# Second-layer routing tables built from one token tile at a time, with four buffers and later matmuls

## The chip, the cores and the metric

The kernel runs on one core of a Trainium2 chip. The metric is the device time of one launch in microseconds (us). The kernel before takes 1202.62 us (median of three runs, 1202.22 to 1203.43).

## The reference

Two transformer layers work on 4 x 512 tokens of width 256, all in float32. Each layer adds an attention part and a mixture-of-experts part, both computed from the same normalised input. The change is in the mixture of experts of the second layer: 7 experts, the best 3 of them for each token.

```python
def _L1_ffn_ref(x, W1, Wg, W2, Ws1, Wsg, Ws2, gate_w, gate_b, biases):
    output = _expert_ffn(x, Ws1, Wsg, Ws2)
    gate_probas = jax.nn.softmax(x @ gate_w + gate_b, axis=-1)
    _, topk_idxs = jax.lax.top_k(gate_probas + biases, TOP_K)
    topk_probas = jnp.take_along_axis(gate_probas, topk_idxs, axis=-1)
    topk_probas = topk_probas / jnp.sum(topk_probas, axis=-1, keepdims=True)
    for e in range(NUM_ROUTED):
        w_e = jnp.sum(topk_probas * (topk_idxs == e), axis=-1)
        output = output + _expert_ffn(x, W1[e], Wg[e], W2[e]) * w_e[..., None]
    return output
...
xn = _layernorm(x, axis=-1)
x = x + _L0_attn_ref(xn, ...) + _L0_ffn_ref(xn, ...)
xn = _layernorm(x, axis=-1)
x = x + _L1_attn_ref(xn, ...) + _L1_ffn_ref(xn, ...)
```

## The kernel before

**Experts by slots.** The 2048 tokens are 16 tiles (NT) of 128. Each token goes to 3 experts (K1), and the rows that go to one expert are packed into slots of 128 rows; there are 54 slots (NS1). Two tables are needed for that: for every slot and lane the number of the token that sits there (from it idx1, the row to gather, and to1, the row to add to) and the share with which its result counts (part1). `route1` (L1460) makes them.

**How the tables are made.** For every pair of a token and one of its three choices, the lane and the slot are known. VectorE compares the lane with 0 to 127 (row, L1538) and the slot with 0 to 53 (the left half of col, L1546). GpSimd multiplies col by the share (right half, L1552) and then by the token's number (left half, L1555). TensorE multiplies row by col and adds all 48 products of 128 x 108 up in one bank, ix (L1529); a product is issued as two matmuls. The kernel before does two token tiles at a time: 8 rounds of 6 products, in two buffers each of row and col; the products of a round are issued one round after its comparisons. At the end VectorE turns ix into the tables (L1561 to L1564).

**The order around it.** The order of the instructions on TensorE, VectorE and ScalarE is written out by hand. From the first attention unit on, the main loop goes over 32 units (4 batches x 8 units), in each over 4 tiles of 128 queries, and for each tile over two half-steps. A half-step issues the two score matmuls of a unit that comes two units later (`score_max`, L940, into the only tile pa), the two score matmuls of this unit (`score`, L979), the row maximum on VectorE (`take_max`, L958), whatever `after` (L832) held back for VectorE, and the exponentials on ScalarE (L994). The first half-step of a tile also issues the products with the values of the tile before (`values`, L1002). I call it an A-half, and the other one a B-half. Then come fillers: pieces of other work, each a generator that yields an estimate of its time.

- While the tables aren't ready, `piece` gives one filler a half-step, and the list todo (with `route1` in it) is advanced by `within`, up to a `yield None`.
- Afterwards `pieces_for` gives fillers by a credit of 0.87 in an A-half and 1.5 in a B-half.
- `slots1` (L1219) is the filler for the experts. For slot s: `tokens(s)` puts a ScalarE copy of the transposed rows, xT (L145), and starts a transposition for slot s+2 on SP's queue and a gather for slot s+4 on GpSimd's queue (L1230); two gate halves (`half`, L1258) in the one bank "g"; their products with the activation on VectorE (L1174, L1175), held back by `after` until the next half-step; two transpositions (`turn_back`, L1240); two down products (`down`, L1271), a ScalarE copy y with the share (L1281), and a GpSimd scatter that adds y to rows in DRAM (L1283). The first gate half of the next slot waits for the step that `behind` (L811) gives: the next A-half.
- `project_out` (L1154) is the attention's output projection, four tiles of two products each (L1138), added by VectorE one half-step later (L1142).
- Fillers other than the gate halves share two banks ("f"); `takes` (L815) hands them out.

**The end.** When the last slot is done, `sums1` (L1338) reads the summed expert rows back (L1350 on GpSimd's queue, which waits for the last scatter), adds them (L1359), and `leaves` (L1146) stores a finished batch (L1151, on SP's queue, which is in order). On the same queue `context` sends the sums of a unit's exponentials away (L1020, L1024) and `quotients` their reciprocals (L1033, L1035) and reads them back spread out (L1039). `closing` (L1044) multiplies with them (L1095 on GpSimd) and makes the last projections (L1106 to L1126).

**Weights.** When `route1` has ended, `expert_weights` loads the last experts' 2304 KB on GpSimd's queue (L762), into the room that the tables were worked out in.

Of the kernel before, what the change touches and what calls it, by code (L numbers as in the profile page):

```python
# [11 lines left out]
F32 = mybir.dt.float32  # L12
# [9 lines left out]
P = 128  # L22
# [9 lines left out]
NT = B * NQ  # L32
# [8 lines left out]
E1, F1, K1 = 7, 256, 3  # L41
W1E = HC * 2 * F1 + HC * H
NS1 = (NT * P * K1 + E1 * (P - 1)) // P
# [5 lines left out]
def two_layer_kernel(  # L49
# [123 lines left out]
    def numbers(pool, n: int):  # L173

        lane = counting(pool, P, 1, 0, "lane")
        slot = counting(pool, n, 1, 0, "slot")
        tok = counting(pool, NT, P, 1, "tok")
        full = counting(pool, NT, P, 0, "full")
        return lane, slot, tok, full, tok[:, 0:1]

    def triangle(pool):

        ones = pool.tile([P, P], F32, tag="ones", name="ones")
        nc.gpsimd.memset(ones, 1.0)
        before = pool.tile([P, P], F32, tag="before", name="before")
        nc.gpsimd.affine_select(
            out=before,
            in_=ones,
            compare_op=ALU.is_gt,
            fill=0.0,  # L190
            base=0,
            pattern=[[1, P]],
            channel_multiplier=-1,
        )
        return ones, before
# [124 lines left out]
    def softmax(lg, n: int, pool, name: str, nq: int = NQ):  # L320

        mx = pool.tile([P, nq], F32, tag="mx", name=f"mx{name}")
        nc.vector.reduce_max(out=mx, in_=lg, axis=AX.X)
        d = pool.tile([P, nq, n], F32, tag="sd", name=f"sd{name}")
        nc.vector.tensor_tensor(d, lg, mx.unsqueeze(2).to_broadcast([P, nq, n]), ALU.subtract)
        nc.scalar.activation(d, d, AF.Exp)
        sm = pool.tile([P, nq], F32, tag="sm", name=f"sm{name}")
        nc.vector.reduce_sum(out=sm, in_=d, axis=AX.X)
        nc.vector.reciprocal(sm, sm)
        return d, sm.unsqueeze(2).to_broadcast([P, nq, n])  # L330
# [12 lines left out]
    with tc.tile_pool(name="w0", bufs=1, side="right") as w0:  # L343
# [37 lines left out]
        with tc.tile_pool(name="rt", bufs=1) as rt, tc.tile_pool(name="a0", bufs=2) as a0, tc.tile_pool(  # L381
            name="a0p", bufs=2, space=PSUM
# [229 lines left out]
            for i in range(NT + 2):  # L612
                b, t = divmod(i, NQ)
# [40 lines left out]
        for i in range(2):  # L654
            k = hp.tile([P, 2, 2, S], F32, tag=f"k{i}", name=f"k1_{i}")
# [22 lines left out]
        with tc.tile_pool(name="m0", bufs=3) as m0, tc.tile_pool(  # L678
            name="m0p", bufs=2, space=PSUM, reuse_waits="tile"
# [113 lines left out]
    with tc.tile_pool(  # L793
        name="a1", bufs=2, side="right", reuse_waits="tile"
    ) as a1, tc.tile_pool(
        name="a1p", bufs=1, space=PSUM, reuse_waits="tile"
    ) as a1p:
        def filler(shape, name: str):

            return a1p.tile(shape, F32, tag="f", name=name, bufs=2)  # L800
# [659 lines left out]
        def route1():  # L1460


            kept = Room(ew, LATE * W1E, E1 * W1E, hp)
            lane, slot, tok, full, own = numbers(kept, NS1)
            toks = kept.tile([P, NT, K1], F32, tag="toks", name="toks1")

            nc.gpsimd.tensor_scalar(
                toks, tok.unsqueeze(2).to_broadcast([P, NT, K1]), 1.0, None, ALU.add
            )
            place1 = kept.tile([P, NT, K1], I32, tag="place1", name="place1")  # L1470
            share1 = kept.tile([P, NT, K1], F32, tag="share1", name="share1")
            spare_row = kept.tile([P, 1], F32, tag="spare", name="spare_row")
            nc.gpsimd.tensor_scalar(spare_row, own, float(NT * P + 1), None, ALU.add)
            for i in range(2):
                kept.tile([P, NT, K1], F32, tag=f"pf{i}", name=f"pf{i}")
            rt = Room(ew, kept.at, E1 * W1E, hp)
            ones, before = triangle(rt)
            yield 0.1
            lb = rt.tile([P, NT, E1], F32, tag="lb", name="lb1")
            nc.vector.tensor_tensor(  # L1480
                lb, va1[:, :, KV1:VG], gb1s.unsqueeze(1).to_broadcast([P, NT, E1]), ALU.add
            )
            e, rs = softmax(lb, E1, rt, "1", NT)
            yield 1.6
            pr = rt.tile([P, NT, E1], F32, tag="pr", name="pr1")
            nc.vector.tensor_tensor(pr, e, rs, ALU.mult)
            pads = 8 - K1
            bp = rt.tile([P, NT, E1 + pads], F32, tag="bp", name="bp1")
            nc.gpsimd.memset(bp[:, :, E1 : E1 + pads], PAD1)
            nc.vector.tensor_tensor(  # L1490
                bp[:, :, 0:E1], pr, eb1s.unsqueeze(1).to_broadcast([P, NT, E1]), ALU.add
            )
            yield 0.6
            mask = yield from top_of(rt, bp, E1, pads, K1, PAD1, PAD1, 4)
            flat = mask.rearrange("p t e -> p (t e)")
            yield 0.3
            pc = filler([P, 2, NT * E1], "cnt1")
            nc.tensor.matmul(pc[:, 0, :], ones, flat, start=True, stop=True)
            nc.tensor.matmul(pc[:, 1, :], before, flat, start=True, stop=True)
            yield None  # L1500
            cnt = rt.tile([P, 2, NT * E1], F32, tag="cnt", name="cnt1s")
            nc.vector.tensor_copy(cnt, pc)
            yield 0.4
            for i, tag in enumerate(("rest", "bp")):
                rt.held["sel", i] = rt.held[tag, 0]
            part = yield from spots(
                rt, kept, E1, K1, W1E, mask, pr, cnt, own, full, place1, share1, off1
            )
            yield 0.9
            while not free:  # L1510
                yield None


            rt = Room(ew, kept.at, E1 * W1E, hp)
            ix = gate_bank([P, 2 * NS1], "ix1")
            n, last = 2 * K1, NT // 2 - 1
            which, rows, toks, parts = (
                x.rearrange("p t k -> p (t k)") for x in (*part, toks, share1)
            )

            def spread(x, t: int, m: int):
                return x[:, ts(t, n)].unsqueeze(2).to_broadcast([P, n, m])

            held = []
            for t in range(last + 2):
                if held:
                    row, col = held.pop()
                    for k in range(n):
                        nc.tensor.matmul(  # L1529
                            ix,  # L1530
                            row[:, k, :],
                            col[:, k, :],
                            start=t == 1 and k == 0,
                            stop=t == last + 1 and k == n - 1,
                        )
                if t <= last:
                    row = rt.tile([P, n, P], F32, tag="row", name=f"row1_{t}", bufs=2)
                    nc.vector.tensor_tensor(  # L1538
                        row,
                        lane.unsqueeze(1).to_broadcast([P, n, P]),  # L1540
                        spread(rows, t, P),
                        ALU.is_equal,
                    )
                    col = rt.tile([P, n, 2 * NS1], F32, tag="col", name=f"col1_{t}", bufs=2)
                    lanes = col[:, :, 0:NS1]
                    nc.vector.tensor_tensor(  # L1546
                        lanes,
                        slot.unsqueeze(1).to_broadcast([P, n, NS1]),
                        spread(which, t, NS1),
                        ALU.is_equal,  # L1550
                    )
                    nc.gpsimd.tensor_tensor(  # L1552
                        col[:, :, NS1:], lanes, spread(parts, t, NS1), ALU.mult
                    )
                    nc.gpsimd.tensor_tensor(lanes, lanes, spread(toks, t, NS1), ALU.mult)  # L1555
                    held.append((row, col))
                    yield 1.1
                    yield None
            number = ix[:, 0:NS1]
            none = rt.tile([P, NS1], F32, tag="none", name="none")  # L1560
            nc.vector.tensor_scalar(none, number, 0.0, spare_row, ALU.is_equal, ALU.mult)  # L1561
            nc.vector.scalar_tensor_tensor(to1, number, -1.0, none, ALU.add, ALU.add)
            nc.vector.tensor_scalar(idx1, number, -1.0, 0.0, ALU.add, ALU.max)
            nc.vector.tensor_copy(part1, ix[:, NS1:])  # L1564
            yield 0.8
# [17 lines left out]
        with tc.manual_schedule(engines={ENG.PE, ENG.DVE, ENG.Activation}):  # L1583
# [57 lines left out]
            for g in range(AHEAD):  # L1641
                b, u = units[g]
                for t in range(NQ):
                    out, pa = banks(b, u, t)
                    for s in range(4):
# [4 lines left out]
                            start=True,  # L1650
                            stop=True,
# [91 lines left out]
            held = {}  # L1743
# [3 lines left out]
            todo, last, urgent = [], [], []  # L1747
# [56 lines left out]
            for g, (b, u) in enumerate(units):  # L1804
# [17 lines left out]
                for t in range(NQ):  # L1822
                    exs = {}
                    if nxt:
                        for first, second in ((0, 2), (2, 0)):
# [18 lines left out]
                            if b == 0:  # L1844
                                chore((last,))
                                n = joined
# [4 lines left out]
                    else:  # L1851
                        chore()
                        out, _ = banks(b, u, t)
                        for s in range(4):
# [4 lines left out]
                                start=True,  # L1859
                                stop=True,  # L1860
# [111 lines left out]
```

## Time and profile before

| what | value |
|---|---|
| median of three runs | 1202.62 us |
| the profiled execution | 1206.58 us |
| its span in the profile | 1204.6 us |
| TensorE matmuls busy | 1118.2 us (93%) |
| VectorE busy | 659.7 us (55%) |
| ScalarE busy | 530.1 us (44%) |
| GpSimd busy | 379.7 us (32%) |
| L1538, 8 times, 594.7 to 620.4 us | 0.948 us each |
| L1546, 8 times | 0.490 us each |
| L1552 and L1555, 8 times each | 0.731 and 0.733 us each |
| L1529, 96 matmuls, 599.4 to 624.8 us | 0.275 us each |
| first and last gate half L1258 | 638.5 and 1149.3 us |

In lines of a timeline the columns are the start and the length in us, the engine (PE is TensorE, PEld its weight loads, DVE VectorE, ACT ScalarE, POOL GpSimd, SPq the instructions that issue DMAs on SP's queue), the line, the operation, what it writes and reads, how many were merged, and in brackets how long the engine was idle just before and what ended that. In a list of waits it is the engine and line that waited, what it waited for, the total in us, how often, and the longest single wait. In a line of a windows view it is the stretch, its length, the busy time of PE, PEld, DVE, ACT and POOL with the number of instructions, then the granted TensorE clock, the busy share of the DMA engines and GB/s.

### The profile page before, as it was taken

What the parts mean: (1) busy time and instruction counts of PE and PEld (TensorE: products, weight loads), DVE (VectorE), ACT (ScalarE), POOL (GpSimd) and SP (SyncE); (2) the same over time, 40 slices, a digit from 0 to 9 for tenths busy, and PEclk for the clock granted to TensorE, in tenths of its full rate; (3) what the DMA queues carried; (4) which work ended last, traced back from release to release, by engine and by line L of the source; (5) the groups of instructions that cost most, each with busy time, mean ns of one, the idle gap of its engine ahead of it and who ended that gap; (6) DMA issues with size and microseconds to landing.
All of it is one profiled execution on the core that took longest, in us unless ns stands there. A gap on an engine that the chain in (4) does not pass through costs nothing.

```text
span 1204.6 us, 17284 instructions
## 1 busy us (share of the span) xinstructions
PE 1118.2 (93%) x5608; PEld 518.4 (43%) x5608; DVE 659.7 (55%) x1329; ACT 530.1 (44%) x1088; POOL 379.7 (32%) x403
## 2 busy tenths in 40 slices
PE   6889989999999988898899999999999999999996
PEld 4456656777765533332243233333233333333333
DVE  3387434444444488757665445555555555555544
ACT  3421233333411103444335545666556566556662
POOL 4400254434334657200042232323133232333140
PEclk9898999999999989899999999999999999999999
DMA  9400268878821322420013332333232323223242
GB/s 355 184 1 1 57 171 187 185 167 178 165 72 57 115 69 85 136 49 9 10 53 100 48 61 44 56 54 57 37 61 52 56 47 60 53 41 53 35 100 64
DMA packets 129863, 101.83 MB, mean 85 GB/s; under 512 B 92048, under 2 KB 117424, under 8 KB 129136
## 3 DMA queue, kind: packets, MB, share of 16 engines
q1 hardware_dynamic: 109296, 58.62, 20.3%
q0 software_dynamic: 19488, 41.70, 15.5%
q8 instruction: 47, 0.77, 0.3%
q10 hardware_dynamic: 992, 0.41, 0.1%
q14 instruction: 40, 0.33, 0.1%
HBM read 51.42 MB, written 26.20 MB: 64 GB/s over the span
## 4 chain that ended last, share of the span: by engine, by line
PE 73%; DVE 15%; DMA 5%; issue 3%; POOL 2%; ACT 1%; SPq 0%; POOLq 0%; ACTq 0%; DVEq 0%
PE pa L940 19%; DVE mx L958 9%; PE po L1002 8%; PE pg L711 7%; PE pg L1258 7%; PE py L735 5%; PE ps L1380 4%; PE py L1271 3%; PE pb L979 2%; PE po L598 2%; PE sc L565 2%; DMA xh<-xg 2%; PE pys L1394 1%; PE pa L727 1%; PE ph L1188 1%
## 5 line engine op out<-in xcount | busy, mean ns | idle before, releaser
L958 DVE TENSOR_REDUCE mx<-pa 128x2 f32<-128x1024 f32 x247 | 302.5, 1225 | 295.8 <-PE pb L979 270.1
L994 ACT ACTIVATE ex<-pb 128x512 f32<-128x512 f32 x496 | 269.6, 595 | 284.9 <-PE pb L979 275.4
L940 PE MATMUL pa<-k,q 32*128 32x512 f32 x960 | 272.1, 643 | 25.7 <-DVE mx L958 20.7
L979 PE MATMUL pb<-q,k 32*128 32x512 f32 x960 | 273.1, 643 | 0.0
L940 PEld LDWEIGHTS pa<-k,q 32*128 32x128 f32 x960 | 72.2, 184 | 162.9 <-DVE mx L958 108.0
L1283 POOL DMA_INDIRECT sum_rows<-y,place x54 | 85.1, 1575 | 166.9 <-ACT y L1281 152.1
L1002 PE MATMUL po<-ex,v 128*32 128x512 f32 x1024 | 137.3, 608 | 0.0
L685 POOL DMA_INDIRECT xg<-xn_rows,idx x79 | 74.9, 948 | 154.1 <-DMA xh<-xg 70.2
L1258 PE MATMUL pg<-ew,xT 128*128 x216 | 116.3, 620 | 3.6 <-ACT xT L145 1.6
L1230 POOL DMA_INDIRECT xg<-xn_rows,idx x54 | 53.9, 998 | 185.9 <-DMA xh<-xg 158.8
L711 PE MATMUL pg<-we,xT 128*128 x316 | 106.9, 460 | 4.3 <-ACT xT L145 4.3
L145 ACT COPY xT<-xh 128x512 uint16<-128x512 uint16 x133 | 89.1, 670 | 15.9 <-DMA xh<-xg 11.2
L735 PE MATMUL py<-we,aT 88*128 x316 | 81.3, 380 | 0.0
L1410 POOL DMA_INDIRECT yk<-y_rows,place x64 | 61.9, 968 | 49.6 <-DVE x L1440 33.5
L979 PEld LDWEIGHTS pb<-q,k 32*128 32x128 f32 x960 | 73.3, 184 | 0.2 <-ACT ex L994 0.2
L722 DVE TENSOR_TENSOR a<-sg,pg 128x176 f32<-128x176 f32 x79 | 26.6, 337 | 83.3 <-ACT sg L720 73.3
L711 PEld LDWEIGHTS pg<-we,xT 128*128 128x128 f32 x316 | 59.4, 190 | 26.9 <-ACT xT L145 5.8
L720 ACT ACTIVATE sg<-pg 128x176 f32<-128x176 f32 x79 | 25.1, 317 | 100.9 <-PE pg L711 83.5
L1271 PE MATMUL py<-ew,aT 128*128 x216 | 65.5, 412 | 0.0
L1002 PEld LDWEIGHTS po<-ex,v 128*32 128x32 f32 x1024 | 20.2, 108 | 98.2 <-issue 96.3
L1271 PEld LDWEIGHTS py<-ew,aT 128*128 128x128 f32 x216 | 35.5, 189 | 57.7 <-issue 30.9
L735 PEld LDWEIGHTS py<-we,aT 88*128 88x128 f32 x316 | 53.7, 190 | 4.6 <-issue 0.2
(262 smaller groups left out, 1380.0 us busy)
## 6 DMA issues: line engine op xcount, KB each, us to landing
y_rows<-y SPq DMA_DIRECT2D x79, 128.0 KB
we<-in_dram SPq DMA_DIRECT2D x4, 2432.0 KB
ew<-in_dram SPq DMA_DIRECT2D x5, 768.0 KB
ew<-in_dram POOLq DMA_DIRECT2D x1, 2304.0 KB
xg<-xn_rows,idx POOLq DMA_INDIRECT x133
xh<-xg SPq DMA_TRANSPOSE x133
x<-in_dram SPq DMA_DIRECT2D x4, 512.0 KB
xn_rows<-xs POOLq DMA_DIRECT2D x16, 128.0 KB
```

Of the source, the lines that this page charges most:

```text
L145: nc.scalar.copy(xT.rearrange("p c t -> p (c t)").bitcast(U16).rearrange("p (c t a) -> p c t a", c=HC, a=2), xh.rearrange("p a c t -> p c ...
L685: nc.gpsimd.indirect_dma_start(out=xg, out_offset=None, in_=xn_rows[:, :], in_offset=bass.IndirectOffsetOnAxis(ap=idx[:, s : s + 1], axis=0),)
L711: nc.tensor.matmul(pg, xT[s][:, c, :], we[:, ds(regs[s] + c * 2 * F0, 2 * F0)], start=c == 0, stop=c == HC - 1,)
L735: nc.tensor.matmul(py, actT[s][0:F0H, j, :], we[0:F0H, ds(regs[s] + HC * 2 * F0 + j * H, H)], start=j == 0, stop=j == 1,)
L940: nc.tensor.matmul(pas[i], q[at : at + ST, u, ts(t, P)], k[at : at + ST, 0, u % 2, :], start=True, stop=True, tile_position=(at, 0),)
L958: nc.vector.reduce_max(out=m[:, s0 : s0 + 2, t], in_=pa, axis=AX.X)
L979: nc.tensor.matmul(pb, k[at : at + ST, 1, u % 2, ts(kc, P)], q[at : at + ST, u, :], start=True, stop=True, tile_position=(at, 0),)
L994: nc.scalar.activation(ex, pb, AF.Exp, scale=1.0 / math.sqrt(D1))
L1002: nc.tensor.matmul(po[ts(s, ST), :], v[:, kc, half * 4 + s, :], exs[s], start=kc == 0, stop=kc == NQ - 1, tile_position=(0, s * ST),)
L1258: nc.tensor.matmul(pg, xT[s][:, c, :], ew[:, ds(regs[s] + c * 2 * F1, 2 * F1)], start=c == 0, stop=c == HC - 1,)
L1271: nc.tensor.matmul(py, x[:, f, :], ew[:, ds(regs[s] + HC * 2 * F1 + f * H, H)], start=f == 0, stop=f == HC - 1,)
L1283: nc.gpsimd.indirect_dma_start(out=sum_rows[:, :], out_offset=bass.IndirectOffsetOnAxis(ap=to1[:, s : s + 1], axis=0), in_=y, in_offset=No ...
```

## The change

The loop goes over 16 single token tiles in place of 8 pairs, with 3 products each. Row and col have four buffers each. The products of tile t are issued in the round of tile t+3, in front of that tile's comparisons, and only every second round ends a half-step (`yield 1.1` and `yield None`). So a half-step issues the products of two tiles and the comparisons of two others. The loop has 19 rounds in place of 9.

```diff
-            n, last = 2 * K1, NT // 2 - 1
+            n, last = K1, NT - 1
...
             held = []
-            for t in range(last + 2):
-                if held:
-                    row, col = held.pop()
+            for t in range(last + 4):
+                if t > 2:
+                    row, col = held.pop(0)
                     for k in range(n):
                         nc.tensor.matmul(
                             ix,
                             row[:, k, :],
                             col[:, k, :],
-                            start=t == 1 and k == 0,
-                            stop=t == last + 1 and k == n - 1,
+                            start=t == 3 and k == 0,
+                            stop=t == last + 3 and k == n - 1,
                         )
                 if t <= last:
-                    row = rt.tile([P, n, P], F32, tag="row", name=f"row1_{t}", bufs=2)
+                    row = rt.tile([P, n, P], F32, tag="row", name=f"row1_{t}", bufs=4)
...
-                    col = rt.tile([P, n, 2 * NS1], F32, tag="col", name=f"col1_{t}", bufs=2)
+                    col = rt.tile([P, n, 2 * NS1], F32, tag="col", name=f"col1_{t}", bufs=4)
...
                     held.append((row, col))
-                    yield 1.1
+                    if t % 2:
+                        yield 1.1
+                if t % 2:
                     yield None
```

## The prediction

> **What bounds the kernel now.** Sums are made on the profiled execution: span 1204.6 us inside 1206.58 us; the runs' median is 1202.62, and the change in microseconds is carried over to it.
>
> The page's chain of the work that ended last comes first: TensorE, with its score line L940, leads it, and DVE is second by the maximum L958, which must leave the one PSUM tile that the next L940 writes.
>
> ```profile
> PE 73%; DVE 15%; DMA 5%; issue 3%; POOL 2%; ACT 1%; SPq 0%; POOLq 0%; ACTq 0%; DVEq 0%
> ```
>
> So I cut the trace into half-steps, from one L940 pair to the next. An A-half also holds the value products L1002, a B-half doesn't; the fillers come on top. Without fillers a half-step never falls under 2.46 us (594.86 to 597.32): L940, then L958, then L940 again. With them TensorE's work decides. The second view is the timeline where the table is built, L1529:
>
> ```profile
> 604.19 0.70 PE L940 MATMUL pa<-k,q 32*128 32x512 f32 x2
> 606.32 1.59 PE L1529 MATMUL ix<-ew 128*128 128x108 f32 x12
> 607.84 0.70 PE L940 MATMUL pa<-k,q 32*128 32x512 f32 x2
> 609.60 1.59 PE L1529 MATMUL ix<-ew 128*128 128x108 f32 x12 [0.62 <-POOL ew L1555]
> 611.12 0.70 PE L940 MATMUL pa<-k,q 32*128 32x512 f32 x2
> ```
>
> The A-half (604.19 to 607.84) is full. The B-half (to 611.12, 3.28 us) waits 0.62 us for GpSimd's L1555. The list of TensorE's waits between 594 and 640 us gives the whole prize:
>
> ```profile
> PE ix L1529 <- POOL ew L1555: 2.5, 4, 0.6
> ```
>
> The 11.0 us that the line's own view shows there are mostly weight loads waiting beside other matmuls.
>
> Third, two misfits in the expert part, when a filler comes a half-step too close to what it needs:
>
> ```profile
> 689.08 0.70 PE L940 MATMUL pa<-k,q 32*128 32x512 f32 x2
> 691.84 0.42 DVE L1175 SCALAR_TENSOR_TENSOR act<-ths,pg 128x256 f32<-128x256 f32 x1
> 692.40 1.10 PE L1258 MATMUL pg<-ew,xT 128*128 x2 [0.46 <-DVE act L1175]
> ...
> 700.53 0.67 ACT L145 COPY xT<-xh 128x512 uint16<-128x512 uint16 x1
> 701.26 1.13 PE L1258 MATMUL pg<-ew,xT 128*128 x2 [0.71 <-ACT xT L145]
> ```
>
> Misfit one: a slot's first gate half stands in the A-half right after the B-half with the previous slot's second; the bank is free only after L958, L1174 and L1175. That A-half takes 4.35 us (689.08 to 693.43; again 4.36 from 707.33), and 3.56 with the same matmuls and an earlier second half (836.96 to 840.52): 0.79 us. Misfit two: L145 is issued in the same B-half as the gate half that reads it. It takes 3.98 us (698.34 to 702.32; again from 902.34) against 2.99 (1083.38 to 1086.37): 0.99 us.
>
> Last, the end:
>
> ```profile
> 1169.83 0.42 SPq L1151 DMA_DIRECT2D out_dram<-x  x1
> 1170.35 0.57 SPq L1020 DMA_DIRECT2D sums<-o  x1
> 1176.34 0.35 DVE L1033 RECIPROCAL sums<-sums 128x32 f32<-128x32 f32 x1 [5.44 <-DMA sums<-o]
> 1182.76 2.33 POOL L1095 TENSOR_TENSOR cr<-cr,den 128x1024 f32<-128x1024 f32 x1 [4.96 <-DMA den<-quot]
> 1185.15 1.34 PE L1106 MATMUL last<-wo1s,cr 128*128 128x256 f32 x4 [2.87 <-POOL cr L1095]
> ```
>
> ```profile
> 1187.00:1189.00 2.00, 2.00 (x9) 0.52 (x8) 0.59 (x2) 0.00 (x0) 0.00 (x0) 0.50 0.00 0
> ```
>
> The store L1151 holds SP's queue until the expert sums are added; L1020 behind it feeds L1033, the quotients, L1095 and L1106. TensorE stands 2.87 us, and the granted clock falls to 0.50 (the last line is of the windows view; the clock is the third number from its end).
>
> **The change, part by part.** The order of instructions of both kernels shows the same 96 table matmuls, spread over nine half-steps (3, seven times 6, 3) in place of eight of 6; every filler after that comes one half-step later; A and B change places for most experts.
>
> *Wait for L1555.* Each half-step now multiplies a token tile that was compared two half-steps before and one that was the first of the last: ready about 1.4 us early. With all four B-halves at 2.66 (3.28 less 0.62): -2.5. The four buffers bring no new wait: the second comparison starts about 3.05 us into an A-half (L958 begins at 1.2 and takes 1.1 from start to start, the first pair 0.7), the product that frees its buffer ends near 2.9.
>
> *Twice as many instructions.* DVE's 768 elements take 0.948 us and 324 take 0.49, so about 0.15 is fixed; from start to start a half-step's four take 1.42 in place of 1.32. With L958 that is 2.6, under the pair's mean of 3.15. GpSimd's 0.73 for 324 elements halves nearly, since its 1024 take 2.33. But GpSimd now multiplies while DVE compares the next tile, which it didn't before. One row shows what that can do: L1086 takes 1.85 us beside L1095, 0.29 otherwise. Bounds: nothing, or two GpSimd multiplications of 0.37 in DVE's way in each half-step, 0.24 to 0.4 per pair beyond the slack, 1.7 in all. I take +0.5, nearer the lower end, since DVE has some 0.5 us to spare per half-step. [...]
>
> *Half-steps' shapes.* Fillers are the same, so only those under 2.46 differ. Pricing each half-step by the trace's shortest of the same contents, the first group of three saves 0.75, the 188 from 624.98 to 1157.65 differ by +0.1, and the last down product L1271 (1.05) falls behind them: +0.4.
>
> *Start of the experts.* The tables are done about 0.5 us earlier, so the first L145 ends near 637.9 in place of 638.46: it waits for its transposition, which shares the DMA engines with the 2304 KB of weights. TensorE gets to the first gate half at 636.7 and waits 1.2 (before: 0.3). +0.95, between 0 and 1.2.
>
> *Misfits.* I list for every slot in which half-step its copy, gate halves and products stand. Before, misfit one comes twice (beside the very first pair of slots, equal in both) and misfit two twice, and these are the slots where the trace has the waits. After: six times (slots 26, 28, 30, 32, 34, 52) and four times (31, 33, 35, 37). Four more at 0.79 and two more at 0.99: +3.2 and +2.0. A third is new: in two places both first output projections (L1138) stand in one B-half and take both filler banks, so the third must wait in the next A-half for L958 and the addition L1142: 1.2 + 1.1 + 0.4 + 0.1 = 2.8 against 2.1. No row shows it: 0 to 0.75 each. The same bank rule costs L1258 in full, so I take 0.7: +1.4.
>
> So far: -2.5 + 0.5 + 0.4 + 0.95 + 3.2 + 2.0 + 1.4 = +5.95.
>
> *The end.* From the start H of the last regular A-half (before 1157.65): the last slot's scatter moves from H+0.5 to H+4.0, since its product now stands behind the A-half's 2.1 us. Its loads and the first eight additions follow 11.6 us later as before, H+15.6. The eight sums and copies now stand before the store on SP and land by H+14.3, so L1033 runs at H+15.7 (before H+18.7). But the quotient is now behind the 512 KB store: traffic after that store lasted 4 us, so H+20.3; the reading back takes up to 4.5 as before, and L1095 2.4: L1106 may go at H+26.4 to 27.3. TensorE is there at H+25.7 (before 24.6). It waits 0.7 to 1.6 in place of 2.87: -1.7. The clock rows 1185 to 1191 (0.74, 0.50, 0.91) cost 0.52 + 1.0 + 0.18 = 1.7; by the stretched matmuls 1.55. A wait of 1.32 us at 597.32 left the clock at 1.00, so the dip goes: -1.55, or nothing. [...]
>
> Sum: +5.95 - 1.7 - 1.55 = +2.7, and 1202.62 + 2.7 = 1205.3 us.
>
> **Rivals.** (1) Faster: the misfits in the expert part cost nothing in the new order, as DVE and ACT run ahead of TensorE there. Without the 6.6 us of misfits 1198.7; it decides once these cost under about 1.5 us. For: the wait on L1555 goes, and the stall at the end. Against: the order shows the same neighbours that cost 0.79 and 0.99 in all four cases of before. (2) No change: the third misfit and the wait at the experts' start don't show: 1205.3 - 1.4 - 0.95 = 1203.0. For: no row shows either. [...] (4) The table wait stays: +2.5, 1207.8; the order speaks against it.
>
> **How the numbers follow.** Forecast 0.46; (1) 0.11; (2) 0.22; (3) 0.14; (4) 0.07. 0.2% is 2.4 us, about what runs between 1202.22 and 1203.43 can tell from no change; the limit is 1205.0, so my forecast lies just beyond it. I give a third of its chance, with (2), to no change: faster 0.11, same 0.37, slower 0.52. The range reaches down by the costs that no row shows (1.4 and 0.95) and the end's remaining wait (1.1), and up to rival 3: 1201.9 to 1209.2.
>
> **What would show it.** [...] L1258 waiting for L1175 in six A-halves and for L145 in four B-halves between 900 and 1150; L1138 waiting for L1142 twice. L1020 ahead of L1151; L1106 waiting under 1.6 us, the clock at 1.00 after it. I am wrong if the misfits are absent while their order stands, or if the end's gain outgrows them.

## The result and the profile after

| | before | after |
|---|---|---|
| median of 22 runs each | 1202.07 us (1197.73 to 1206.06) | 1206.06 us (1201.86 to 1208.05) |
| ratio after to before | | 1.003, 95% interval 1.0021 to 1.0039 |
| profiled execution, its span | 1206.58, 1204.6 us | 1206.52, 1204.7 us |

The change costs 4.0 us by the medians. The two profiled executions are level only by chance: they differ by 3.48 us before the change begins (the first half-step to start after the first comparison has begun starts at 594.86 before, at 591.38 after). The page's chain of the work that ended last reaches back only to 1159.08 us in the changed kernel, about 4% of the span, and can't be set beside the one of before. So I count from that half-step on, in half-steps from one first L940 pair to the next. The boundaries are read from the timelines: 12 half-steps of table building, 6 with the gate halves of the first two slots, 180 to the last score pair L940, and the rest.

| stretch | before | after | difference | the prediction's terms |
|---|---|---|---|---|
| first comparisons, 12 half-steps | 38.83 | 35.40 | -3.43 | -2.5 + 0.5 - 0.75 = -2.75 |
| the next 6, start of the experts | 18.27 | 22.17 | +3.90 | +0.95 |
| the next 180, the misfits and L1271 | 507.76 | 514.85 | +7.09 | 3.2 + 2.0 + 1.4 + 0.1 + 1.05 = +7.75 |
| from there to the end of the span | 44.88 | 40.90 | -3.98 | -1.7 - 1.55 = -3.25 |
| sum | 609.74 | 613.32 | +3.58 | +2.7 |

First the tables, in TensorE's timeline of the changed kernel (start, duration, engine and line, what it writes and reads, then any wait in brackets):

```profile
601.75 1.59 PE L1529 MATMUL ix<-ew 128*128 128x108 f32 x12
603.27 0.70 PE L940 MATMUL pa<-k,q 32*128 32x512 f32 x2
...
604.34 1.59 PE L1529 MATMUL ix<-ew 128*128 128x108 f32 x12
605.86 0.70 PE L940 MATMUL pa<-k,q 32*128 32x512 f32 x2
...
607.92 1.59 PE L1529 MATMUL ix<-ew 128*128 128x108 f32 x12
609.44 0.70 PE L940 MATMUL pa<-k,q 32*128 32x512 f32 x2
```

No bracket is left: the 0.62 us for L1555 is gone. From 603.27 to 605.86 a B-half takes 2.59 us where it took 3.28, and the A-half to 609.44 takes 3.58.

Then TensorE's list of waits from 560 us on (what waited, for whom, sum in us, times, the longest):

```profile
PE pg L1258 <- ACT xT L145: 6.4, 6, 2.3
PE pg L1258 <- ACT y L1281: 2.8, 5, 0.6
...
PE po L1138 <- DVE x L1142: 1.3, 2, 0.6
...
PE pg L1258 <- DVE act L1175: 0.5, 1, 0.5
```

These are the misfits: 5 + 1 of the first kind, four of the six waits for L145 of the second, two of the third. One of each kind in the timeline:

```profile
904.73 0.42 DVE L1175 SCALAR_TENSOR_TENSOR act<-ths,pg 128x256 f32<-128x256 f32 x1
904.78 0.47 ACT L1281 ACTIVATE y<-py,share 128x256 f32<-128x256 f32 x1 [0.50 <-PE py L1271]
...
905.30 1.10 PE L1258 MATMUL pg<-ew,xT 128*128 x2 [0.56 <-ACT y L1281]
```

```profile
892.98 0.74 DVE L1142 TENSOR_TENSOR x<-x,po 128x256 f32<-128x256 f32 x2
...
893.44 1.13 PE L1138 MATMUL po<-wo1s,cr 128*128 128x256 f32 x4 [0.65 <-DVE x L1142]
...
948.39 1.13 PE L1258 MATMUL pg<-ew,xT 128*128 x2 [0.71 <-ACT xT L145]
```

The bracket at 905.30 names L1281, but L1281 reads the filler bank, not the gate bank. L1175, which frees the gate bank, ends at 905.15, and L1258 starts 0.15 us later, as it does where L1175 is named (939.54, L1175 ended 939.40). The half-steps around these waits last 4.36, 3.84 and 3.97 us.

The other two of the six waits for L145 stand at the start of the experts:

```profile
635.77 3.14 PE L1258 MATMUL pg<-ew,xT 128*128 x4 [2.27 <-ACT xT L145]
...
642.74 1.13 PE L1258 MATMUL pg<-ew,xT 128*128 x2 [1.28 <-ACT xT L145]
```

The windows view of the same place (stretch, its length, busy time of PE, PEld, DVE, ACT and POOL, then the granted clock, the DMA share and GB/s):

```profile
636.00:637.00 1.00, 1.00 (x3) 0.26 (x3) 0.00 (x0) 0.70 (x2) 0.67 (x1) 0.73 0.16 23
637.00:638.00 1.00, 1.00 (x3) 0.33 (x1) 0.00 (x0) 0.00 (x0) 0.61 (x1) 0.50 0.62 120
638.00:639.00 1.00, 1.00 (x6) 0.17 (x5) 0.00 (x0) 0.06 (x1) 0.88 (x2) 0.50 0.62 143
639.00:640.00 1.00, 1.00 (x8) 0.35 (x8) 0.00 (x0) 0.33 (x1) 0.08 (x1) 0.57 0.49 141
```

TensorE waits 2.27 us, and 0.7 us after the wait's end the clock falls to half for 3.4 us. That is why these four matmuls take 3.14 us; in the first experiment, at a clock of 1.00, they take 1.98.

And the end, in the timeline:

```profile
1173.47 0.54 SPq L1020 DMA_DIRECT2D sums<-o  x1
...
1176.18 0.35 DVE L1033 RECIPROCAL sums<-sums 128x32 f32<-128x32 f32 x1
...
1176.29 0.42 SPq L1151 DMA_DIRECT2D out_dram<-x  x1
...
1176.90 0.38 SPq L1035 DMA_DIRECT2D quot<-sums  x1
...
1180.75 1.58 SPq L1039 DMA_DIRECT2D den<-quot  x4
...
1184.78 2.36 POOL L1095 TENSOR_TENSOR cr<-cr,den 128x1024 f32<-128x1024 f32 x1 [5.83 <-DMA den<-quot]
...
1187.20 1.13 PE L1106 MATMUL last<-wo1s,cr 128*128 128x256 f32 x4 [0.25 <-POOL cr L1095]
```

L1020 now stands ahead of the store L1151, L1033 no longer waits, the quotient L1035 is behind the store, and L1106 waits 0.25 us in place of 2.87. The clock stays at 1.00.

### The profile page after: what moved, and what is told of

The parts are those of the page before. It is cut to its first block, busy times and chain, and to the rows that moved or that the text cites. A ratio compares the mean times of both kernels' runs of the same rounds, so it can differ in the third digit from the quotient of the medians.

```text
span 1204.7 us, 17332 instructions
## 1 busy us (share of the span) xinstructions
PE 1116.8 (93%) x5608; PEld 518.4 (43%) x5608; DVE 663.3 (55%) x1345; ACT 530.8 (44%) x1088; POOL 384.7 (32%) x419
## 5 line engine op out<-in xcount | busy, mean ns | idle before, releaser
L940 PE MATMUL pa<-k,q 32*128 32x512 f32 x960 | 272.3, 642 | 26.2 <-DVE mx L958 23.3
L940 PEld LDWEIGHTS pa<-k,q 32*128 32x128 f32 x960 | 72.5, 184 | 161.3 <-DVE mx L958 111.9
L1002 PE MATMUL po<-ex,v 128*32 128x512 f32 x1024 | 136.4, 605 | 0.0
L1258 PE MATMUL pg<-ew,xT 128*128 x216 | 118.0, 629 | 9.7 <-ACT xT L145 6.4
L145 ACT COPY xT<-xh 128x512 uint16<-128x512 uint16 x133 | 89.1, 671 | 19.1 <-DMA xh<-xg 14.3
L1271 PE MATMUL py<-ew,aT 128*128 x216 | 65.8, 410 | 0.0
L1002 PEld LDWEIGHTS po<-ex,v 128*32 128x32 f32 x1024 | 20.1, 108 | 97.4 <-issue 95.6
L1271 PEld LDWEIGHTS py<-ew,aT 128*128 128x128 f32 x216 | 35.7, 188 | 58.4 <-issue 35.2
L1258 PEld LDWEIGHTS pg<-ew,xT 128*128 128x128 f32 x216 | 33.5, 189 | 59.1 <-issue 22.3
```

The lines of the kernel that those rows point to most:

```text
L145: nc.scalar.copy(xT.rearrange("p c t -> p (c t)").bitcast(U16).rearrange("p (c t a) -> p c t a", c=HC, a=2), xh.rearrange("p a c t -> p c ...
L940: nc.tensor.matmul(pas[i], q[at : at + ST, u, ts(t, P)], k[at : at + ST, 0, u % 2, :], start=True, stop=True, tile_position=(at, 0),)
L1002: nc.tensor.matmul(po[ts(s, ST), :], v[:, kc, half * 4 + s, :], exs[s], start=kc == 0, stop=kc == NQ - 1, tile_position=(0, s * ST),)
L1258: nc.tensor.matmul(pg, xT[s][:, c, :], ew[:, ds(regs[s] + c * 2 * F1, 2 * F1)], start=c == 0, stop=c == HC - 1,)
L1271: nc.tensor.matmul(py, x[:, f, :], ew[:, ds(regs[s] + HC * 2 * F1 + f * H, H)], start=f == 0, stop=f == HC - 1,)
```

## The experiments

The runs of before beside the experiments had medians from 1198.86 to 1204.27 us, by chip, so only ratios are compared between groups. Unless another count is given, figures "from the first comparisons" are spans from that half-step on, as in the table above (before 609.74, after 613.32). What the expectations call the lock is a slowing in the changed kernel's trace: DVE's L1546 takes 0.58 us where GpSimd's L1552 runs beside it (600.59 us) and 0.32 where it doesn't (599.89 us). How the two engines get in each other's way no run shows.

**One added half-step on the kernel before.**

```
             for t in range(last + 2):
...
+            yield None
             number = ix[:, 0:NS1]
```

> The kernel before with one thing added: an empty half-step between the last table product and the reading of the table. Tables as before (pairs of tiles, two buffers), but every filler behind them in exactly the half-steps of the changed kernel. Theory (the shift costs, the smaller comparisons gain): the wait for L1555 stays (+2.5 against the changed kernel), the lock and the later start of the first products go (-0.8), an extra half-step with hardly any filler (+0.4), so the changed kernel's 1206.1 plus about 2, 1208 us; six waits of L1258 for L1175, four for L145 and two of L1138 for L1142 between 890 and 1150 us. Rival (the cost is in the twice as many instructions, and the shift is paid for by the end): 1201 to 1203 us, level with before.

Measured: 1206.03 us, ratio 1.0027 (1.0011 to 1.0043). From the first comparisons 613.85, within 0.6 us of the changed kernel's 613.32. Two lines of its timeline:

```profile
605.99 1.59 PE L1529 MATMUL ix<-ew 128*128 128x108 f32 x12 [0.62 <-POOL ew L1555]
...
637.30 1.98 PE L1258 MATMUL pg<-ew,xT 128*128 x4 [1.17 <-ACT xT L145]
```

The tables still wait for L1555, and yet the kernel is as slow as the changed one. All twelve misfits are there: the two timelines drift from that of before by 7.09 and 7.46 us over the 180 half-steps. So the loss is the shift by one half-step, not the smaller comparisons. The 2 us I gave it on top of the changed kernel fell short to 0.5, because the experts' first wait is 1.17 us instead of 2.27 and the clock stays up: tables that are done later lose less there (1.7 us of it is the clock's fall, which the second execution of the changed kernel, further down, doesn't have).

**Products two tiles behind, three buffers: the tables alone.**

```
-            for t in range(last + 4):
-                if t > 2:
+            for t in range(last + 3):
+                if t > 1:
...
-                            start=t == 3 and k == 0,
-                            stop=t == last + 3 and k == n - 1,
+                            start=t == 2 and k == 0,
+                            stop=t == last + 2 and k == n - 1,
...
                     if t % 2:
                         yield 1.1
-                if t % 2:
-                    yield None
+                        yield None
```

> The changed kernel with the products two tiles behind the comparisons in place of three (three buffers), so that the tables take eight half-steps as before and every filler stands where it stood before. Theory: the gain of the tables alone, -2.5 for the wait on L1555, +0.5 for the lock, +0.35 for the first products: 1.5 to 2 us below before, about 1200.4 us; no new waits in the expert part, the 2.87 us at L1106 as before. Rival (the smaller instructions cost more than the wait): 1203 us or more, with the half-steps of the tables as long as before or longer.

Measured: 1200.04 us, ratio 0.9984 (0.9972 to 0.9996). Its timeline is 1.77 us ahead of before's after twelve half-steps, 1.56 after 24 and 1.40 at the last score pair; the misfits are before's, the first L1258 waits 0.43 us, and L1106 waits 2.68 us. This is what the smaller comparisons and the later products are worth when no filler moves.

**The changed kernel with one more half-step.**

```
             for t in range(last + 4):
...
+            yield None
             number = ix[:, 0:NS1]
```

> The changed kernel with one more empty half-step before the table is read: fillers two half-steps later than before, so the same ones fall into A- and B-halves nearly as before. By its order misfit one then comes once in place of six times, misfit two twice in place of four times, misfit three once in place of twice; and the quotient stands before the store on SP. Theory: -4.0 - 2.0 - 0.7 for the misfits, +0.5 for the extra half-step, so about 6 us under the changed kernel, 1200 us, though it starts its experts still later. Rival (the lateness itself costs, or the smaller instructions): 1206 us or more.

Measured: 1196.33 us, ratio 0.9951 (0.9933 to 0.997), well beyond the 6 us expected. From the first comparisons 605.13, 8.2 us under the changed kernel: 3.2 at the start (L1258 waits 0.68 and then 1.19 us, the clock stays at 1.00), 6.3 in the 180 half-steps, and 1.3 given back at the end, where L1106 waits 1.04. I had counted the misfits and left out the start. Being later is no loss by itself; it matters which half the fillers fall in.

**The store on another queue, in the kernel before.**

```
-                    (step + 4, lambda: nc.sync.dma_start(out=out_view[b], in_=xs[b]))
+                    (step + 8, lambda: (nc.sync if b else nc.scalar).dma_start(out=out_view[b], in_=xs[b]))
```

> The kernel before with the first of the three late stores (L1151, the one that holds SP's queue until the expert sums are added) issued by ACT a few steps later. Nothing else moves. Theory (the store holds L1020, L1033, the quotient, L1095 and L1106): L1020 about 3.5 us earlier, the 2.87 us at L1106 and the clock's fall gone, -3 to -4.4, about 1198 us. Rival (another chain, the quotient's way through memory, ends as late): 1201 to 1203 us with L1106 waiting over 2 us.

Measured: 1197.55 us, ratio 0.9959 (0.9944 to 0.9974). From the timeline:

```profile
1166.64 0.35 DVE L1033 RECIPROCAL sums<-sums 128x32 f32<-128x32 f32 x1 [0.28 <-DMA sums<-o]
...
1173.82 0.41 ACTq L1151 DMA_DIRECT2D out_dram<-x  x1
...
1177.70 1.13 PE L1106 MATMUL last<-wo1s,cr 128*128 128x256 f32 x4
```

L1106 waits for nothing. Up to the last score pair the timeline is before's within 0.1 us, and the rest takes 40.28 in place of 44.88: the store's place on SP was worth 4.6 us, 2.87 of waiting and 1.7 of clock. The edit also has all three stores issued four steps later; what the other queue gives and what the later step gives isn't told apart.

**GpSimd's multiplications put behind both tiles in the program: no test.** Both tiles' multiplications were written behind the second tile's comparisons.

```
-                    nc.gpsimd.tensor_tensor(
...
+                    pair.append((t, col, lanes))
+                    for at, c, lanes in pair if t % 2 else ():
+                        nc.gpsimd.tensor_tensor(
...
```

> The changed kernel with GpSimd's four multiplications of a half-step issued together behind the comparisons of both token tiles, so that the first two no longer run while DVE compares the second tile. Theory (the lock is there, L1546 0.58 instead of 0.32 beside a multiplication, but DVE has time to spare): L1546 0.32 throughout, the half-steps of the tables as in the changed kernel, 2.59 and 3.58 us, its time level with the changed kernel's 1206 within 1.5 us. Rival (the lock takes part of the gain): the first half-step falls from 2.80 to 2.46, others with it, 1 us or more in all, 1205 us or less.

Measured: ratio 1.0023 (1.0004 to 1.0043). The order on GpSimd's own queue is the same as before the edit, and its first multiplication waits only for the first tile, so the overlap stayed:

```profile
596.42 0.58 DVE L1546 TENSOR_TENSOR ew<-ew 128x162 f32<-128x162 f32 x1
```

```profile
596.18 0.64 POOL L1554 TENSOR_TENSOR ew<-ew 128x162 f32<-128x162 f32 x1 [0.80 <-DVE ew L1546]
```

It is a repetition of the changed kernel and says nothing on what the overlap costs; the last experiment does. At the start its first L1258 waits 2.09 us and the clock falls; at the end L1106 waits 0.37 us and it doesn't.

**Only the misfits taken out, from slot 20 on.**

```
             for s in range(NS1 + 1):
+                if s in (20,):
+                    yield None
```

> The changed kernel with one empty half-step ahead of expert slot 20: the tables and the start of the experts are untouched, and from slot 20 on the fillers are back in halves of the same kind as before. By its order none of the six misfits one, none of the four misfits two and none of the two misfits three is left behind slot 20. Theory: -6 x 0.79 - 4 x 0.99 - 2 x 0.7 + 1.5 for the empty half-step, 8.5 us under the changed kernel, 1197.5 us; the waits of L1258 for L145 at the start stay. Rival (the misfits are hidden by other waits, the loss is at the start and in the tables): 1203 us or more.

Measured: 1196.43 us, ratio 0.9976 (0.9958 to 0.9994), so 2.4 us under its before; from the first comparisons 607.30, 6.0 under the changed kernel in place of 8.5. All that its list of waits has for L1258 over 0.4 us, and the line of L1106:

```profile
PE pg L1258 <- ACT xT L145: 3.4, 2, 2.1
...
PE last L1106 <- POOL cr L1095: 0.8, 1, 0.8
```

The two waits at the start remain, and all twelve misfits are gone: the 180 half-steps take 508.42 us in place of 514.85, 6.4 less. With the 1.5 us that the empty half-step costs by my count, the misfits were worth 7.9 and not 10.1. They are the loss, but I had priced them too high.

**The weights behind the first three gathers on GpSimd's queue.**

```
                 yield from route1()
-                expert_weights(LATE, E1 - LATE, nc.gpsimd)
...
             gather(3)
+            expert_weights(4, E1 - 4, nc.gpsimd)
```

> The changed kernel with the 2304 KB of expert weights issued behind the first three gathers on GpSimd's queue in place of behind the first one. TensorE's order is the same. Theory (the second gather stands behind the weights, and the first L145 runs only when that gather's transposition has landed): L145 5 us earlier, L1258's first wait (2.27) gone and the second (1.28) shorter, the clock at 1.00 there, 2 to 4 us under the changed kernel, 1202 to 1204 us. Rival (TensorE's first gate half must have the weights themselves): it waits for the weights instead, as long or up to 2 us longer, 1206 to 1208 us.

Measured: ratio 1.0015 (1.0001 to 1.0029), from the first comparisons 611.77, 1.6 us under the changed kernel.

```profile
622.66 0.95 POOL L1230 DMA_INDIRECT xg<-xn_rows,idx  x1 [0.30 <-PE pb L979]
...
623.62 0.61 POOL L762 DMA_DIRECT2D ew<-in_dram  x1
629.18 0.68 ACT L145 COPY xT<-xh 128x512 uint16<-128x512 uint16 x1
...
633.08 1.96 PE L1258 MATMUL pg<-ew,xT 128*128 x4 [1.82 <-DMA ew<-in_dram]
```

Both expectations are half right. Counted from the first comparisons, L145 runs 3.6 us earlier (40.05 against 43.66), so the second gather, which had stood behind the weights, had held it. But L1258 then waits 1.82 us for the weights themselves. The wait is 0.45 us shorter and the clock stays at 1.00, and of the 2.11 us saved by the end of these gate halves the clock is the larger part, 1.66. That part isn't shown to come from the edit: the unchanged kernel's second execution keeps its clock too, and against that one the edit saves 0.43 us here.

**Both gains together.** The edits of the products two tiles behind and of the store.

> The products two tiles behind the comparisons (fillers where they stood before) together with the store issued by ACT. Theory (the table's gain and the end's gain are at different places and add up): -1.9 - 4.6 from the two traces, 6.5 us under before, 1195.5 us. Rival (a gain in one place is taken back in the other): 1198 us or more.

Measured: 1192.2 us against 1198.86, ratio 0.9945 (0.9924 to 0.9966), 6.7 us. They add up; L1106 has no wait.

**The same with two slots moved.** Ahead of slots 5 and 26 (`if s in (5, 26): yield None`).

> Products two tiles behind, the store issued by ACT, and a filler left out once ahead of slots 5 and 26, which takes misfit one from slot 5 and misfit two from slot 26 by its order. Theory: the time of the products two tiles behind with the store moved (ratio to before 0.9945), less 0.79 and 0.78, at no more half-steps: 0.993, about 8 us under before. Rival (the leftover half-step returns it): 0.9945 or more.

Measured: 1190.74 us against 1199.2, ratio 0.993 (0.9909 to 0.9951), as expected; the interval still holds the 0.9945 of the version without the slots. The timelines from the first comparisons, 601.67 against 602.70, speak for it. This is the fastest version tried.

**One more half-step and the store moved.** The edits of the third and fourth experiments.

> The changed kernel with the extra half-step ahead of the table's reading, and the store issued by ACT. Theory: in the trace with the extra half-step L1106 waited 1.0 us without a fall of the clock, and this wait goes: ratio to before 0.994 in place of 0.995. Rival (ACT's queue is held by the store, whose sums come later here): 0.996 or more, with ACT waiting ahead of the last exponentials.

Measured: ratio 0.9944 (0.9926 to 0.9962). L1106's wait is down to 0.11 us and ACT isn't held, as expected, but 0.9951 lies in the interval too: by the ratios alone this step is not settled. The timelines, 604.4 against 605.1, speak for a small gain.

**The changed kernel again.**

> The changed kernel unchanged, beside the two above on one chip. Theory: ratio to before 1.002 to 1.004; in its profile the same misfits and the same waits at the start, 2.1 to 2.3 and 1.28 us; the clock falls behind the first of them if the wait is over 2.1 us.

Measured: 1202.63 against 1199.2 us, ratio 1.0025 (1.0009 to 1.004). The same twelve misfits, but this timeline differs at both ends:

```profile
630.81 1.98 PE L1258 MATMUL pg<-ew,xT 128*128 x4 [2.22 <-ACT xT L145]
...
1181.95 1.82 PE L1106 MATMUL last<-wo1s,cr 128*128 128x256 f32 x4 [1.59 <-POOL cr L1095]
```

```profile
1182.00:1183.00 1.00, 1.00 (x3) 0.87 (x4) 0.71 (x3) 0.00 (x0) 0.00 (x0) 0.62 0.00 0
1183.00:1184.00 1.00, 1.00 (x4) 0.72 (x3) 0.00 (x0) 0.00 (x0) 0.00 (x0) 0.50 0.34 114
```

At the start the clock stays at 1.00 although the wait is 2.22 us, against my expectation; at the end it falls after 1.59 us. The start costs 2.21 us instead of 3.90, and the end gives 0.99 instead of 3.98. From the first comparisons it takes 614.62. So 1.7 us of every gain at the start that was counted against the first execution is the clock's fall there: beside this one, the start takes 1.05 us less in the first experiment, 1.55 in the third and 0.43 with the weights moved.

**GpSimd over both tiles at once: no overlap.**

```
-                    nc.gpsimd.tensor_tensor(
-                        col[:, :, NS1:], lanes, spread(parts, t, NS1), ALU.mult
-                    )
...
+                    if t % 2:
+                        lanes = both[:, :, 0:NS1]
+                        nc.gpsimd.tensor_tensor(
+                            both[:, :, NS1:], lanes, spread2(parts, t // 2), ALU.mult
+                        )
...
```

> The changed kernel with GpSimd's multiplications over both token tiles of a half-step at once (324 elements, eight pairs of instructions in place of sixteen), so that the first can't begin before DVE's last comparison has ended. DVE and TensorE do the same in the same order. Theory (the lock is real but DVE has time to spare): DVE's second L1546 at 0.32 in place of 0.58, GpSimd's two at 0.73, the tables' half-steps at TensorE's 2.6 and 3.6 us as before, the first one between 2.46 and 2.80; at most 0.4 us from the lock, ratio to before 1.002 to 1.004. Rival (the lock takes a part of the gain that counts): the first twelve half-steps at least 1 us under the changed kernel's 35.4.

Measured: 1206.75 against 1204.27 us, ratio 1.0023 (1.0009 to 1.0037). From its timeline (L1538 is L1541 here, L1546 is L1551, L1552 is L1559):

```profile
592.02 0.32 DVE L1551 TENSOR_TENSOR ew<-ew 128x162 f32<-128x162 f32 x1
592.48 0.73 POOL L1559 TENSOR_TENSOR ew<-ew 128x324 f32<-128x324 f32 x1 [26.98 <-DVE ew L1551]
```

No multiplication runs beside the second comparison, which takes 0.32 us in place of 0.58, and the first half-step falls from 2.80 to 2.54 us: the overlap cost 0.26. But GpSimd's results come later again, and the twelve half-steps take 36.81 in place of 35.40. The 1.41 us lost there come back in the next six and more, 19.72 in place of 22.17: L1258's first wait is 1.45 in place of 2.27 and the clock stays up (beside the second execution, 20.48, it is 0.76 that comes back). The half-steps of the tables didn't stay as short as I expected, yet the ratio is that of the changed kernel.

## Why the prediction came out right, point by point

The forecast of 2.7 us more stands beside 4.0 measured; the cause it named is the one that the runs show. The kernel before with the late fillers alone is as slow as the changed one (ratio 1.0027), and the tables without the late fillers are faster than before (0.9984). But the sum came out with luck: the start of the experts was priced 2.95 us too low, and the tables, the misfits and the end came out 0.68, 0.66 and 0.73 us better than priced, so that most of the one miss is covered. In the changed kernel's second execution the start was priced 1.3 us too low and the end's gain 2.3 us too high.

*Wait for L1555, half-steps' shapes, twice as many instructions:* the B-halves took 2.59 us where 2.66 was forecast, and DVE's slowing beside GpSimd cost 0.26 us where I took 0.5 and bounded it by 1.7: each second L1546 takes 0.26 us longer, but TensorE shows it in the first half-step alone. The twelve half-steps gained 3.43 us, forecast 2.75. DVE's L1538 took 0.55 to 0.66 us; the second L1546 shows the slowing more plainly (0.58 against 0.32). GpSimd's multiplication did not halve: 0.46 for 162 elements where 0.73 was for 324. It didn't matter.

*Start of the experts* is the term that was mis-sized: +0.95 forecast, with 1.2 as the upper bound for the wait; +3.90 in the profiled execution. I had the first wait at 1.2 and it is 2.27. Before, the weights' load, the first L145 and the first gate half are

```profile
627.12 0.61 POOL L762 DMA_DIRECT2D ew<-in_dram  x1
...
637.78 0.68 ACT L145 COPY xT<-xh 128x512 uint16<-128x512 uint16 x1 [1.78 <-DMA xh<-xg]
...
638.50 1.13 PE L1258 MATMUL pg<-ew,xT 128*128 x2 [0.22 <-ACT xT L145]
```

and in the changed kernel, ahead of the wait of 2.27 us,

```profile
625.28 0.60 POOL L762 DMA_DIRECT2D ew<-in_dram  x1 [1.95 <-issue]
...
635.04 0.68 ACT L145 COPY xT<-xh 128x512 uint16<-128x512 uint16 x1 [3.50 <-DMA xh<-xg]
```

Counted from 594.86 and 591.38, TensorE comes to its first gate half 1.30 us earlier than before (42.12 against 43.42). But L762, and with it the second gather behind it, leaves 1.64 us later (33.90 against 32.26), and L145 ends 0.74 us later (44.34 against 43.60) where I had it 0.5 us earlier. With before's 0.22 (I had read 0.3) this is the 2.27. What holds L762 for 1.95 us the profile doesn't name, and it stays open. I also left out that the second slot's wait grows (1.28, where before had 0.98 for L1175), and above all that the clock can fall there. The pieces nearly meet the row: 2.27 + 1.28 + 1.70 (0.27, 0.50, 0.50 and 0.43 lost in the four windows) - 0.22 - 0.98 = 4.05. The second execution, where the clock held, has +2.21. And the step's picture was not complete: the first gate half needs the weights too. With L145 early it waits 1.82 us for the load. So within six half-steps all of the 3.4 us gained is lost again, in the second execution 2.2 of them. That isn't the price of being early alone: with the products two tiles behind, 1.56 of the 1.77 us gained came through this stretch.

*Misfits:* six, four and two, at the slots that were named. Misfit one's half-steps last 4.36 us as before, and misfit three's 3.84, 0.71 more than the matmuls in them add up to (1.07 for the scores, 1.0 for L1002, 2 x 0.53 for L1138): both prices hold. Misfit two was too dear. I compared its 3.98 us with a half-step of 2.99; two L1271, one L1258 and the two pairs of scores add up to 2 x 0.53 + 1.06 + 1.07 = 3.19, so it costs 0.78, not 0.99. The 180 half-steps cost +7.09 in place of +7.75.

*The end:* the mechanism is as described (L1020 ahead of the store, the quotient behind it). L1106's wait was to be 0.7 to 1.6 us; it was 0.25 in one execution and 1.59 in the other. Moving the store by itself gave 4.6 us, which fits the price of wait and clock (2.87 and 1.7). But that the clock would hold after a shorter wait is not sure: in the second execution it fell after 1.59 us, and the end gave 0.99 us in place of 3.98.

*Rivals.* (1) falls: the misfits show in full and the kernel gains 6.4 us when they are taken out. (2) falls: both terms show, the start above its bound. (3), from which the range has its 1209.2 us, is half true in a single execution, where the end waits 1.59 us and the clock falls; but the 1209.2 takes DVE's slowing beside GpSimd at the bound of 1.7 us, which no run shows: it cost 0.26. (4) falls, no wait for L1555 is left.

What stays open: how often the clock falls at the start and how often at the end. With the two runs that leave the start as it is (the repetition with GpSimd's multiplications, and the one changed from slot 20 on) it fell at the start in three of four profiled executions; at the end, in one of the three that leave the end as it is. The medians will hold a mixture.

## What to carry to other kernels

In a kernel whose fillers sit in alternating slots, a change that adds one slot moves all work behind it, and the order of instructions tells which neighbours then come too close; before costing the change itself, list them, and compare each with a half-step that holds the very same matmuls. Ask also what the sped-up stage feeds, and follow that chain by itself: here the weights and the second gather left 1.64 us later, and TensorE, being early, only waited longer. Test the parts apart: here the gain in the tables (0.9984) and the moved store (0.9959) were worth more than 6 us together, and the shift that came with the change hid the first of them.

## What the runs showed of the hardware

Length alone doesn't decide whether the clock falls after a wait of TensorE. The same wait of 2.07 to 2.08 us at L1188, ahead of everything that was changed, is followed by half clock in 7 of the 14 profiled executions and by full clock in the other 7. After waits of 2.27, 2.11 and 2.09 us at the experts' start it fell, after 2.22, 1.82 and 1.45 it didn't; at the end it fell after 2.87, 2.68 and 1.59 us, and not after 1.04 or less. Each of these falls lasts 3.4 us at 0.50 and costs 1.7 us, whatever the wait was.

In three traces the stretches of half clock start whole steps of 3.413 us apart: before, at 486.21, 578.37 and 1185.94 us, 27 and 178 steps; in the changed kernel at 575.01 and 636.45 us, 18 steps; with the products two tiles behind at 575.72 and 1179.88 us, 177 steps. Cut by these steps, the seven waits at L1188 that were followed by half clock have 1.83 to 2.08 us in the one step ahead of the fall. In the changed kernel's second execution, counted back from its fall at 1182.24 us, the wait at L1188 is cut into 1.60 and 0.47 us and the one of 2.22 us into 0.69 and 1.53, and the clock stayed up after both. So the outcome seems to go with where a wait lies as well. That is my reading of these rows; no run shows why, and the rows give no clean bound: 1.59 us in a single step (L1106 in the second execution) was followed by half clock, 1.66 us (L940 in the changed kernel, up to 594.18 us) was not, and in the changed kernel 1.29 us of idle TensorE in the step ahead of 428.24 us was, for 10.2 us.

DVE and GpSimd slow each other where they overlap in the changed kernel's tables: DVE's comparison of 162 elements (L1546) takes 0.58 us beside a multiplication and 0.32 without one, and GpSimd's multiplication of 162 (L1552) takes 0.64 us beside the second tile's comparisons (600.35 us) and 0.46 behind them (601.48 us).
